# Gathers for three instead of four destination tiles in the second attention layer, with a ring of eight row sets

## The chip, the cores and the metric

The kernel runs on one core of a Trainium2 chip. The metric is the device time of one execution in microseconds (us); of several executions the median is given. The profile is one further execution, recorded by the hardware profiler. Its engines are PE (matrix products, with PEld for the loading of weights), DVE (vector), ACT (scalar), POOL (GpSimd) and SP, which only issues transfers.

## What is computed

A graph of 3125 nodes with 256 features and 103125 edges, sorted by destination, goes through four blocks in float32: three attention layers over the graph, a layer of 16 experts, a sum over neighbours, and a layer of 8 experts. The change touches the second of the three attention layers. One such layer is

```python
h = x @ W
el = h @ al
er = h @ ar
e = leaky_relu(el[src] + er[dst], 0.2)
m = segment_max(e, dst)
ex = exp(e - m[dst])
alpha = ex / segment_sum(ex, dst)[dst]
out = segment_sum(alpha[:, None] * h[src], dst) + b      # relu after layers 1 and 2
```

so every destination node takes a weighted mean of the rows of `h` of its source nodes.

## The kernel before

The nodes are cut into 25 tiles of 128 (the last has 53). The kernel has two ways to make the weighted sums of a layer.

The dense way serves all destinations of layers 1 and 3, and most of layer 2. The number of edges between each source and each destination lies in a table `counts`. Destinations are taken in parts of 256 (`PARTS_OF`; the last part has 53), and for each part the loop over `s` goes through the 25 source tiles. In step `s` DVE makes `pm` (L1575), the 128 x 256 weights of this source tile for these destinations, and PE multiplies each half of it with the 257 columns of `h` (features and the sum of weights) into `acc` (L1578), one matmul for each destination tile. The `pm` tiles come from a pool of six buffers. The part of 53 destinations has its own form (L1566, L1570). When a part is done, `divide` (L1610) makes the mean of it, and `onward_steps` (L1468) turns the result (L1474, L1476), multiplies it with the next layer's weights (L1345) and keeps it (L1352): a part's closing work is done by events placed in the steps of the next part.

The other way is `Apart` (L2050), used in layer 2 for the first destinations, here four tiles (0 to 3, 512 nodes). During layer 1 each row of `h` is also saved to a table in DRAM (L2063). For every destination the list of its sources lies in order in the edge list, so POOL fetches with one indirect transfer the j-th source row of 128 destinations at once: one row set of 128 x 258 values. A destination has 38 such slots (`OWN`), and up to 128 destinations with more edges get 20 extra ones (`HEAVY`), which are done first. DVE adds a row set times a coefficient into `apart_acc` (L2200); the coefficients of a batch of four slots come from one small instruction (L2191), which reads the four row sets. At the end of a tile the sums of the extra slots are handed out by a matmul (`expand`, L2205) and added (`gather`, L2209), and the tile goes onward as the others do.

Layer 2 is written out by hand in order (`manual_schedule`, L1527), so what stands before what on an engine is what the loops say. PE, DVE, ACT and POOL each run their own instructions in order. The parts of the layer are `NEXT_PARTS` (L1267): ten parts of 256 and the one of 53, and each engine's share of the gathers is laid into their steps by a plan: `events` (L2174) makes a list of pairs, a step number and what to do there. `at(q)` (L2179) turns the time of slot `q`, which is `LANDED + EVERY * q` (19.0 and 1.31 us), into a step, counting 0.976 us for a full step and 0.25 for one of the small part. The main loop runs the events that are due at the end of each step (L1593).

The row sets live in a ring of five buffers of four (`RING`). Five batches are fetched in one go at step 11 (L1588). After that a batch is fetched by four gathers, once the last slot of a batch has been added and has freed its buffer (L2218).

Around the change, SP carries in layer 2 only the saving of rows and weights for later, and POOL the gathers and a few small copies before and after them. Layer 3 begins with source tile 4 (L1573), so the rows of tiles 0 to 3 are wanted last.

Of the kernel before, what the change touches and what calls it, by code (L numbers as in the profile page):

```python
# [22 lines left out]
P = 128  # L23
# [1240 lines left out]
SOME = 6  # L1264
ROW = D + 2
APART = 2
NEXT_PARTS = PARTS_OF[APART:11] + PARTS_OF[12:] + PARTS_OF[11:12]  # L1267
FEW = 2 * APART
OWN = 38
HEAVY = 20  # L1270
SLOTS_OF = [(FEW, HEAVY)] + [(t, OWN) for t in range(FEW)]
BATCH_OF = 4
BATCHES_OF = [(t, k, min(BATCH_OF, n - k)) for t, n in SLOTS_OF for k in range(0, n, BATCH_OF)]
RING = 5
LANDED = 19.0
FETCH = 11
BEGIN = 0
RANK = [(5, 0), (5, 4), (5, 6), (5, 9), (5, 14), (5, 17), (6, 8)]
EVERY = 1.31
STEP, LAST_STEP = 0.976, 0.25  # L1280
HELD = 64.0


# [75 lines left out]
def dense_attention(tc, dram, counts, x_in, big, ident, eps, layers, src, dst, rows, high, make_router, over, count,  # L1359
# [11 lines left out]
    with tc.tile_pool(name="dw", bufs=1) as cp, tc.tile_pool(name="dwl", bufs=2) as wl, \  # L1371
# [3 lines left out]
        with tc.tile_pool(name="dp", bufs=6) as pmp, tc.tile_pool(name="ds", bufs=2) as sp, \  # L1375
# [120 lines left out]
            for i in range(3):  # L1496
# [14 lines left out]
                if apart_now:  # L1511
                    hold = ExitStack()
                    hp = hold.enter_context(tc.tile_pool(name="hp", bufs=1))
                    raws[0] = hp
                    hq = hold.enter_context(tc.tile_pool(name="hq", bufs=1, space=PSUM))
                    def finished(t, acc, b=bt_i, nxt=nxt, w=we_n):
                        col = hp.tile([P, 1], F32, name="apart_col", bufs=2)
                        nc.vector.tensor_scalar(col, acc[:, D:], 1e-30, None, op0=OP.max)
                        nc.vector.reciprocal(col, col)
                        nc.vector.scalar_tensor_tensor(acc[:, :D], acc[:, :D], col, b, op0=OP.mult, op1=OP.add)  # L1520

                        soon.extend(onward_steps(now_step[0] + 1, lambda: acc, t, P, "yT1", nxt, w, None))

                    now_apart += apart.events(finished)
                order = ExitStack()
                if apart_now:
                    order.enter_context(tc.manual_schedule())  # L1527
# [1 line left out]
                for here, (a, c, n) in enumerate(parts):  # L1529
                    tiles = [(q, (c + q) // P, min(P, n - q)) for q in range(0, n, P)]  # L1530
                    following = parts[here + 1:here + 2]
                    short = bool(following) and following[0][2] <= P // 2

                    edges = counts_of(counts, a)
                    if c > GROUPS[a][0]:
# [12 lines left out]
                    for s in range(NT):  # L1548
                        now_step[0] = here * NT + s
                        if s == (EARLIER if apart_now else TERMS):  # L1550
                            if following:
                                tau_next = terms(now, following[0])
                            else:
                                tau_next = None if last else terms(nxt, PARTS_OF[0 if apart_now else APART])
                        if i == 0 and (a, s) in FINISH:
                            locator.finish(FINISH.index((a, s)) + 1, pp)
                        if i == 0 and (a, s) in FIND:
                            locator.find(FIND.index((a, s)) + 1, kp, tau[:, 0:1])
                        later.sort(key=lambda e: e[0])
                        while later and later[0][0] <= s:  # L1560
                            later.pop(0)[1]()
                        if n <= P // 2:
                            if s % SOME == 0:
                                m = min(SOME, NT - s)
                                few = sp.tile([P, SOME, n], F32, name="few")
                                nc.vector.tensor_tensor(few[:, :m], tau[:, None, :n].to_broadcast([P, m, n]),  # L1566
                                                        now.rho[:, s:s + m, None].to_broadcast([P, m, n]), op=OP.max)
                                nc.vector.tensor_tensor(few[:, :m], few[:, :m], edges[:, s:s + m, :n], op=OP.mult)
                            at = s % 2 * (P // 2)
                            nc.tensor.matmul(acc[at:at + n, 0, :D + 1], few[:, s % SOME], now.h[:, s, :D + 1], start=(s < 2),  # L1570
                                             stop=(s >= NT - 2))
                        else:
                            of = (s + FEW) % NT if last and a == 0 else s  # L1573
                            pm = pmp.tile([P, PAIR], F32, name="pm")
                            nc.vector.scalar_tensor_tensor(pm[:, :n], tau[:, :n], now.rho[:, of:of + 1],  # L1575
                                                           edges[:, of, :n], op0=OP.max, op1=OP.mult)
                            for j, (q, t, r) in enumerate(tiles):
                                nc.tensor.matmul(acc[:r, j, :D + 1], pm[:, q:q + r], now.h[:, of, :D + 1], start=(s == 0),  # L1578
                                                 stop=(s == NT - 1))
                        if last and (a, s) == (2, 0):  # L1580
                            during(expert.a[:, 0, 0:1])
                        while ready and ready[0][0] <= s:
                            counter.add(kp, ready.pop(0)[1])
                        if i == 0 and (a, s) in prepare:
                            prepare[a, s]()
                        if apart_now and (a, s) == (APART, BEGIN):
                            apart.begin(hp, hq, pp, now.lr)
                        if apart_now and (a, s) == (APART, FETCH):  # L1588
                            for b in range(RING):
                                apart.fetch(b)  # L1590
                        while soon and soon[0][0] <= now_step[0]:
                            soon.pop(0)[1]()
                        while now_apart and now_apart[0][0] <= now_step[0]:  # L1593
                            now_apart.pop(0)[1]()
                        if s == 2 and fills:

                            for e in empties:
                                nc.gpsimd.tensor_scalar(e, tau[:, 0:1], 0.0, None, op0=OP.mult)
                        if s % 8 == 2 and fills:
                            fills.pop(0)()  # L1600
                        if ahead and s % 3 == 0:
                            counter.make(ahead[0], ACT_OH, tau[:, 0:1] if a == 0 and s < 6 else None)
                            ready.append((s + 2, ahead.pop(0)))
# [446 lines left out]
class Apart:  # L2050
# [86 lines left out]
    def begin(self, hp, hq, pp, lr):  # L2137
# [2 lines left out]
        numbers = hp.tile([P, P], F32, name="numbers")  # L2140
        nc.gpsimd.iota(numbers, pattern=[[1, P]], base=0, channel_multiplier=0, allow_small_or_imprecise_dtypes=True)
        self.numbers = numbers
        hot = hp.tile([P, BATCH_OF, ROW], F32, name="apart_row", bufs=RING)
        hot = hot.rearrange("p j f -> p (j f)")[:, :FEW * P].rearrange("p (t j) -> p t j", j=P)
        self.hots(hot)
        self.back = hp.tile([P, FEW, P], F32, name="hotT")
        ps = pp.tile([P, FEW, P], F32, name="ps_m")
# [11 lines left out]
        for t, n in SLOTS_OF:  # L2159
            nc.vector.tensor_scalar(self.real[:, c:c + n], numbers[:, :n], self.ends[:, t, 1:2], None, op0=OP.is_lt)  # L2160
            c += n
        self.ring = {}

    def fetch(self, b):
        nc = self.nc
        row = self.hp.tile([P, BATCH_OF, ROW], F32, name="apart_row", bufs=RING)
        q = sum(m for _, _, m in BATCHES_OF[:b])
        for j in range(BATCHES_OF[b][2]):
            nc.gpsimd.indirect_dma_start(  # L2169
                out=row[:, j], out_offset=None, in_=self.table[:, :],  # L2170
                in_offset=bass.IndirectOffsetOnAxis(ap=self.who[:, q + j:q + j + 1], axis=0))
        self.ring[b] = row

    def events(self, finished):  # L2174

        nc, made = self.nc, []
        state = {}

        def at(q):  # L2179
            time, steps = LANDED + EVERY * q, 0  # L2180
            for _, _, n in NEXT_PARTS:
                step = STEP if n > P // 2 else LAST_STEP
                if time < NT * step:
                    break
                time, steps = time - NT * step, steps + NT
            return steps + math.ceil(time / step)

        def batch(b, t, q, m):
            row = state["row"] = self.ring.pop(b)
            co = state["co"] = self.hp.tile([P, BATCH_OF], F32, name="apart_co", bufs=2)  # L2190
            nc.vector.scalar_tensor_tensor(co[:, :m], row[:, :m, D + 1], self.tau[:, t:t + 1], self.real[:, q:q + m],  # L2191
                                           op0=OP.max, op1=OP.mult)
# [14 lines left out]
        def gather(t):  # L2207
            acc = state["acc"]
            nc.vector.tensor_tensor(acc, acc, state["ps"], op=OP.add)  # L2209
            finished(t, acc)  # L2210

        q = 0
        for b, (t, k, m) in enumerate(BATCHES_OF):
            made.append((at(q + m), lambda b=b, t=t, q=q, m=m: batch(b, t, q, m)))
            for j in range(m):
                made.append((at(q + m + j), lambda j=j, first=(k + j == 0): slot(j, first)))
            if b + RING < len(BATCHES_OF):
                made.append((at(q + m + m - 1), lambda b=b: self.fetch(b + RING)))  # L2218
            if t < FEW and k == 20:
                made.append((at(q + m + m - 1), lambda t=t: expand(t)))  # L2220
            q += m
            if k + m == dict(SLOTS_OF)[t]:
                if t == FEW:
                    made.append((at(q + m - 1), lambda: state.update(heavy=state["acc"])))
                else:
                    made.append((at(q + m - 1), lambda t=t: gather(t)))
        return made


def spare_rows(tc, cp, rows0, rows1):  # L2230
# [148 lines left out]
```

## Time and profile before

| | |
|---|---|
| median of 3 runs | 1810.56 us (1809.9 to 1813.63) |
| the profiled execution, its own time | 1872.49 us |
| its span, first to last instruction | 1870.8 us |
| PE busy | 1768.7 us, 95% of the span |
| DVE busy | 1021.9 us, 55% |
| POOL busy | 488.6 us, 26% |
| mean granted clock of PE | 0.979 |
| gathers of layer 2 (L2169) | 172, 176.1 us busy on POOL |
| additions of row sets (L2198, L2200) | 172, of which 167 of 482 ns in the median |

The page of a profile gives for each engine how long it was busy, and the span in slices. Groups of instructions have a line of the kernel, an engine, an operation, what it writes and reads, a count, the busy time, the mean duration, and what ended the idle time before them. The view of waits says who waited for whom and for how long; the timeline lists instructions in order. A matmul of float32 leaves two records. The granted clock is the share of full speed that PE was allowed.

### The profile page before, as it was taken

What the parts mean: (1) busy time and instruction counts of PE and PEld (TensorE: products, weight loads), DVE (VectorE), ACT (ScalarE), POOL (GpSimd) and SP (SyncE); (2) the same over time, 40 slices, a digit from 0 to 9 for tenths busy, and PEclk for the clock granted to TensorE, in tenths of its full rate; (3) what the DMA queues carried; (4) which work ended last, traced back from release to release, by engine and by line L of the source; (5) the groups of instructions that cost most, each with busy time, mean ns of one, the idle gap of its engine ahead of it and who ended that gap; (6) DMA issues with size and microseconds to landing.
All of it is one profiled execution on the core that took longest, in us unless ns stands there. A gap on an engine that the chain in (4) does not pass through costs nothing. (4 is left out here: it accounts for less than half of the span.)

```text
span 1870.8 us, 27224 instructions
## 1 busy us (share of the span) xinstructions
PE 1768.7 (95%) x9196; PEld 1380.7 (74%) x9196; DVE 1021.9 (55%) x2933; ACT 727.8 (39%) x2079; POOL 488.6 (26%) x634
## 2 busy tenths in 40 slices
PE   6999999999698978999999999999989999999997
PEld 4788888887586866788887866666668887455786
DVE  6888888875476756777777842222244222333221
ACT  3766667671011111122222322121127999455221
POOL 4210110000566656123333333333310000122121
PEclk9999999999799989999999999999989999999999
DMA  4111123757323322211111177876430000723884
GB/s 116 33 38 56 61 68 136 311 225 300 81 77 82 84 74 79 91 38 46 46 46 41 46 223 195 234 195 194 111 88 1 1 1 1 236 116 154 265 293 124
DMA packets 123716, 215.45 MB, mean 115 GB/s; under 512 B 14811, under 2 KB 86657, under 8 KB 123528
## 3 DMA queue, kind: packets, MB, share of 16 engines
q1 hardware_dynamic: 85860, 137.38, 21.7%
q0 software_dynamic: 24704, 56.84, 11.5%
q10 hardware_dynamic: 12994, 19.29, 3.1%
q8 instruction: 79, 1.29, 0.3%
q14 instruction: 79, 0.65, 0.1%
HBM read 122.54 MB, written 92.61 MB: 115 GB/s over the span
## 5 line engine op out<-in xcount | busy, mean ns | idle before, releaser
L1578 PE MATMUL acc<-big,pm 128*128 128x257 f32 x3400 | 800.1, 386 | 18.9 <-issue 9.1
L1578 PEld LDWEIGHTS acc<-big,pm 128*128 128x128 f32 x3400 | 634.0, 192 | 113.3 <-DVE pm L1575 14.1
L1575 DVE SCALAR_TENSOR_TENSOR pm<-tau,big,counts 128x256 f32<-128x256 f32 (+1 forms) x875 | 400.3, 476 | 144.4 <-PE acc L1578 113.4
L2169 POOL DMA_INDIRECT apart_row<-apart_rows,apart_who x172 | 176.1, 1024 | 115.3 <-DVE apart_acc L2200 53.6
L1778 PE MATMUL acc<-msg,cr 128*128 128x512 f32 (+1 forms) x625 | 157.9, 404 | 0.0
L891 PE MATMUL ps_h<-xsT,w 128*128 128x384 f32 x448 | 147.3, 487 | 0.0
L1778 PEld LDWEIGHTS acc<-msg,cr 128*128 128x128 f32 (+1 forms) x625 | 114.7, 185 | 29.2 <-ACT cr L1774 1.2
L1774 ACT ACTIVATE cr<-counts 128x256 fp32r<-128x256 uint8 (+1 forms) x325 | 130.6, 402 | 13.6 <-PE acc L1778 6.8
L2035 ACT CAST counts<-acc_c 128x500 uint8<-128x500 f32 (+1 forms) x155 | 95.9, 677 | 95.0 <-PE acc_c L2025 94.7
L891 PEld LDWEIGHTS ps_h<-xsT,w 128*128 128x128 f32 x448 | 84.7, 190 | 58.0 <-issue 1.9
L2010 DVE TENSOR_TENSOR ohk<-iota_k,key 128x2016 f16<-128x2016 f16 (+1 forms) x79 | 94.3, 1194 | 20.2 <-PE acc_c L2025 20.0
L1345 PE MATMUL ps_m<-we,yT 128*128 128x258 f32 (+1 forms) x248 | 72.9, 415 | 31.3 <-ACT yT L1476 23.8
L894 ACT ACTIVATE silu<-ps_h 128x384 f32<-128x384 f32 x60 | 29.4, 490 | 170.4 <-PE ps_h L891 168.3
L2004 ACT ACTIVATE ohs<-iota_s,low 128x128 f16<-128x128 f16 x286 | 94.1, 401 | 0.0
L1056 PE MATMUL ps_H<-big,t_w 128*128 128x512 f32 (+1 forms) x224 | 93.1, 552 | 0.8 <-ACT H L1058 0.5
L1476 ACT ACTIVATE yT<-ps_m 128x256 f32<-128x256 f32 (+1 forms) x24 | 9.0, 374 | 212.4 <-remote 99.8
L895 DVE TENSOR_TENSOR hid<-silu,ps_h 128x384 f32<-128x384 f32 x60 | 33.2, 553 | 104.7 <-PE ps_h L891 104.7
L911 POOL DMA_INDIRECT sums<-y,who x45 | 70.0, 1556 | 72.9 <-DVE y L909 64.0
L1184 PE MATMUL ps_y<-t_wd,hsT 128*128 x384 | 87.1, 379 | 0.4 <-ACT hsT L1232 0.4
L2025 PEld LDWEIGHTS <-ohs 128*128 128x128 f16 x1250 | 77.7, 98 | 10.9
L2025 PE MATMUL acc_c<-ohk,ohs 128*128 128x125 f16 x1250 | 84.5, 218 | 0.0
L1345 PEld LDWEIGHTS ps_m<-we,yT 128*128 128x128 f32 (+1 forms) x248 | 45.9, 199 | 49.4 <-ACT yT L1476 26.8
(424 smaller groups left out, 2245.7 us busy)
## 6 DMA issues: line engine op xcount, KB each, us to landing
rows<-empty SPq DMA_DIRECT2D x16, 2564.0 KB
big<-in_L_ffn_w_dram SPq DMA_DIRECT2D x36, 512.0 KB
w<-in_L_ffn_w_dram ACTq DMA_DIRECT2D x36, 512.0 KB
hs<-rows SPq DMA_DIRECT2D x23, 641.0 KB
rows<-empty SPq DMA_DIRECT2D x16, 516.0 KB
t_wd<-in_L_ffn_Wd_dram SPq DMA_DIRECT2D x8, 1024.0 KB
big<-in_L_ffn_Wd_dram SPq DMA_DIRECT2D x6, 1024.0 KB
xs<-rows SPq DMA_DIRECT2D x14, 387.0 KB
```

The source lines that it names most:

```text
L891: nc.tensor.matmul(ps, w[:, k, j * P:(j + 1) * P], xsT[:, k], start=(k == 0), stop=(k == KD - 1))
L1056: nc.tensor.matmul(ps[:, :n], a[:, k, j * P:(j + 1) * P], xnT[:, k, c:c + n], start=(k == 0), stop=(k == KD - 1))
L1345: nc.tensor.matmul(ps[:r], xT[:, k], w[:, k], start=(k == 0), stop=(k == KD - 1))
L1575: nc.vector.scalar_tensor_tensor(pm[:, :n], tau[:, :n], now.rho[:, of:of + 1], edges[:, of, :n], op0=OP.max, op1=OP.mult)
L1578: nc.tensor.matmul(acc[:r, j, :D + 1], pm[:, q:q + r], now.h[:, of, :D + 1], start=(s == 0), stop=(s == NT - 1))
L1774: nc.scalar.activation(cr[:, :n], edges[:, s, :n], AF.Copy, accum_out=seen[:, a * NT + s:a * NT + s + 1])
L1778: nc.tensor.matmul(acc[:r, j].rearrange("p h d -> p (h d)"), cr[:, q:q + r], msg[:, s].rearrange("p h d -> p (h d)"), start=(s == 0), stop ...
L2004: nc.scalar.activation(far[:, i], self.iota_s, AF.Abs, scale=-1.0, bias=self.low32[:, batch, i:i + 1])
L2010: nc.vector.tensor_tensor(to[:, i:tiles].rearrange("p t (x u) -> p t x u", u=2), iota.rearrange("p (x u) -> p x u", u=2)[:, None].to_broad ...
L2025: nc.tensor.matmul(acc[:, u], ohs[:, i], ohk[:, i, :KEYS], start=(t == 0), stop=(t == TW - 1))
L2035: nc.scalar.copy(to[:, :, d0 % PAIR:d0 % PAIR + whole * WIN].rearrange("p s (u d) -> p u s d", u=whole), acc[:, :whole])
L2169: nc.gpsimd.indirect_dma_start(out=row[:, j], out_offset=None, in_=self.table[:, :], in_offset=bass.IndirectOffsetOnAxis(ap=self.who[:, q ...
```

## The change

Three tiles are fetched for (0 to 2, 384 nodes) in place of four. Tile 3 becomes a part of its own of 128 destinations, which layer 2 takes on the dense way as its second part: 25 steps with a half-wide `pm` and one matmul each. `FOLLOWED` names the extra slots and the first three tiles, so there are 134 gathers and additions, not 172, in 35 batches, not 45. The lists of sources and what is prepared from them still cover four tiles.

The ring becomes one tile with places for two batches (eight row sets, before twenty). The first eight row sets are no longer fetched in one go: each has an event of its own from step 11 on, `EVERY` apart, and behind a POOL copy of one column of the latest `pm` into `pace`, which holds it until that product has been made. Every later row set is fetched by an event right after the addition that frees its place, for the batch after the next; the last addition of a batch fetches what is left. The plan changes with it: `LANDED` 16.5, `EVERY` 1.74, and 0.3 us for a step of the 128-wide part. `made` is kept from running out of order, and the first fetches are sorted into it. The closing work of a part that the 128-wide part follows is placed as it is before the part of 53 (`short`).

```diff
-NEXT_PARTS = PARTS_OF[APART:11] + PARTS_OF[12:] + PARTS_OF[11:12]
+NEXT_PARTS = PARTS_OF[APART:APART + 1] + [(1, 3 * P, P)] + PARTS_OF[APART + 1:11] + PARTS_OF[12:] + PARTS_OF[11:12]
...
-BATCHES_OF = [(t, k, min(BATCH_OF, n - k)) for t, n in SLOTS_OF for k in range(0, n, BATCH_OF)]
-RING = 5
-LANDED = 19.0
+FOLLOWED = SLOTS_OF[:4]
+BATCHES_OF = [(t, k, min(BATCH_OF, n - k)) for t, n in FOLLOWED for k in range(0, n, BATCH_OF)]
+RING = 2
+LANDED = 16.5
...
-EVERY = 1.31
-STEP, LAST_STEP = 0.976, 0.25
+EVERY = 1.74
+STEP, HALF_STEP, LAST_STEP = 0.976, 0.3, 0.25
...
-                    now_apart += apart.events(finished)
+                    now_apart += apart.events(finished, lambda: pm[:, 0:1])
...
-                    short = bool(following) and following[0][2] <= P // 2
+                    short = bool(following) and following[0][2] <= (P if apart_now else P // 2)
...
-                        if apart_now and (a, s) == (APART, BEGIN):
+                        if apart_now and (here, s) == (0, BEGIN):
                             apart.begin(hp, hq, pp, now.lr)
-                        if apart_now and (a, s) == (APART, FETCH):
-                            for b in range(RING):
-                                apart.fetch(b)
...
-        hot = hp.tile([P, BATCH_OF, ROW], F32, name="apart_row", bufs=RING)
-        hot = hot.rearrange("p j f -> p (j f)")[:, :FEW * P].rearrange("p (t j) -> p t j", j=P)
+        self.rows = hp.tile([P, RING * BATCH_OF, ROW], F32, name="apart_row")
+        hot = self.rows.rearrange("p j f -> p (j f)")[:, :FEW * P].rearrange("p (t j) -> p t j", j=P)
...
-    def fetch(self, b):
+        self.pace = hp.tile([P, 1], F32, name="pace")
+
+    def of(self, b):
+        at = b % RING * BATCH_OF
+        return self.rows[:, at:at + BATCHES_OF[b][2]]
+
+    def fetch(self, b, j, behind=None):
         nc = self.nc
-        row = self.hp.tile([P, BATCH_OF, ROW], F32, name="apart_row", bufs=RING)
-        q = sum(m for _, _, m in BATCHES_OF[:b])
-        for j in range(BATCHES_OF[b][2]):
-            nc.gpsimd.indirect_dma_start(
-                out=row[:, j], out_offset=None, in_=self.table[:, :],
-                in_offset=bass.IndirectOffsetOnAxis(ap=self.who[:, q + j:q + j + 1], axis=0))
-        self.ring[b] = row
+        if behind is not None:
+            nc.gpsimd.tensor_copy(self.pace, behind)
+        q = sum(m for _, _, m in BATCHES_OF[:b]) + j
+        nc.gpsimd.indirect_dma_start(
+            out=self.of(b)[:, j], out_offset=None, in_=self.table[:, :],
+            in_offset=bass.IndirectOffsetOnAxis(ap=self.who[:, q:q + 1], axis=0))
+
+    def first(self, b, j, recent):
+        self.fetch(b, j, recent())
...
+        first = [(when(FETCH * STEP + g * EVERY),
+                  lambda b=g // BATCH_OF, j=g % BATCH_OF: self.first(b, j, recent)) for g in range(RING * BATCH_OF)]
         q = 0
         for b, (t, k, m) in enumerate(BATCHES_OF):
             made.append((at(q + m), lambda b=b, t=t, q=q, m=m: batch(b, t, q, m)))
+            ahead = range(BATCHES_OF[b + RING][2] if b + RING < len(BATCHES_OF) else 0)
             for j in range(m):
                 made.append((at(q + m + j), lambda j=j, first=(k + j == 0): slot(j, first)))
-            if b + RING < len(BATCHES_OF):
-                made.append((at(q + m + m - 1), lambda b=b: self.fetch(b + RING)))
+                for h in (ahead[j:j + 1] if j < m - 1 else ahead[j:]):
+                    made.append((at(q + m + j), lambda b=b, h=h: self.fetch(b + RING, h)))
...
-        return made
+        for k in range(1, len(made)):
+            made[k] = max(made[k][0], made[k - 1][0]), made[k][1]
+        return sorted(first + made, key=lambda e: e[0])
```

More of the change, by code (lines that the diff above doesn't have):

```diff
@@ L2161, in begin, with events @@
             c += n
-        self.ring = {}
-    def fetch(self, b):
-        nc = self.nc
-        row = self.hp.tile([P, BATCH_OF, ROW], F32, name="apart_row", bufs=RING)
-        q = sum(m for _, _, m in BATCHES_OF[:b])
-        for j in range(BATCHES_OF[b][2]):
-            nc.gpsimd.indirect_dma_start(
-                out=row[:, j], out_offset=None, in_=self.table[:, :],
-                in_offset=bass.IndirectOffsetOnAxis(ap=self.who[:, q + j:q + j + 1], axis=0))
-        self.ring[b] = row
-    def events(self, finished):
+        self.pace = hp.tile([P, 1], F32, name="pace")
[3 more added lines that the diff above has]
+    def fetch(self, b, j, behind=None):
+        nc = self.nc
+        if behind is not None:
[6 more added lines that the diff above has]
+        self.fetch(b, j, recent())
+    def events(self, finished, recent):
         nc, made = self.nc, []
@@ L2179, in at, with when @@
         def at(q):
-            time, steps = LANDED + EVERY * q, 0
+            return when(LANDED + EVERY * q)
+        def when(time):
+            steps = 0
             for _, _, n in NEXT_PARTS:
-                step = STEP if n > P // 2 else LAST_STEP
+                step = STEP if n > P else HALF_STEP if n > P // 2 else LAST_STEP
                 if time < NT * step:
@@ L2188, in batch @@
         def batch(b, t, q, m):
-            row = state["row"] = self.ring.pop(b)
+            row = state["row"] = self.of(b)
             co = state["co"] = self.hp.tile([P, BATCH_OF], F32, name="apart_co", bufs=2)
```

## The prediction

> **What bounds the kernel now.** I read first the busy time of the engines stage by stage: the three attention layers are 72 to 448, 456 to 786 and 786 to 1078 us of the span. Columns: length, then busy us (instructions) of PE, PE weight loads, DVE, ACT and POOL, granted clock, DMA share, GB/s.
>
> ```profile
> 72.00:448.00 376.00, 373.16 (x2651) 321.59 (x2649) 305.33 (x585) 246.76 (x643) 32.72 (x44) 1.00 0.37 139
> 456.00:786.00 330.00, 279.98 (x1264) 229.16 (x1263) 214.37 (x588) 40.39 (x140) 180.09 (x186) 0.93 0.28 77
> 786.00:1078.00 292.00, 289.34 (x1446) 246.64 (x1446) 220.85 (x814) 69.93 (x141) 87.31 (x171) 1.00 0.17 53
> ```
>
> Layers 1 and 3 are full on PE at full clock. Layer 2, the one that the change touches, leaves PE idle for 50 us and has a mean clock of 0.93. No other stage has a gap like it, so next comes the unit of PE work, from the chain that ended last (layer 3), and then the layer's gathers (count, then least, median and most ns, first and last start).
>
> ```profile
> 1063.44 5.65 PE acc L1578 x26
> ```
>
> ```profile
> L2169 POOL DMA_INDIRECT apart_row<-apart_rows,apart_who x172: 951/957/1287, 474.8 to 754.5; - x172
> L2200 DVE SCALAR_TENSOR_TENSOR apart_acc<-apart_row,apart_co,apart_acc x167: 469/482/533, 483.7 to 776.9; 128x257 f32<-128x257 f32 x167
> ```
>
> 26 records take 5.65 us, 0.217 each, and a matmul leaves two: 0.434 us for one destination tile and one source tile. At that price layer 2 is 250 full steps x 2 x 0.434 = 217, the 25 steps of the 53-wide part 10.9, onward work of 25 tiles (4 matmul records and 2 transposes of 0.109) 27, tau terms and the start 7: about 262 us of PE work in 330. The loss is 68.
>
> Where it sits is in the waits of this layer (us in total, times, longest) and the timeline of one stall.
>
> ```profile
> POOL apart_row L2169 <- DVE apart_acc L2200: 53.6, 16, 7.6
> ...
> PE ps_m L1345 <- ACT yT L1476: 23.8, 7, 7.3
> ...
> PE acc L1578 <- issue: 9.1, 4, 4.3
> ...
> PE acc L1578 <- DVE pm L1575: 7.0, 5, 3.6
> ```
>
> ```profile
> 721.00 0.38 PE L1474 MATMUL ps_m<-ident,y 128*128 128x128 f32 x2
> ...
> 721.22 1.03 PE L1578 MATMUL acc<-big,pm 128*128 128x257 f32 x4
> ...
> 726.06 0.95 POOL L2169 DMA_INDIRECT apart_row<-apart_rows,apart_who  x1 [0.30 <-issue]
> 729.10 0.38 ACT L1476 ACTIVATE yT<-ps_m 128x256 f32<-128x256 f32 x1 [11.57 <-remote]
> ...
> 729.53 2.09 PE L1345 MATMUL ps_m<-we,yT 128*128 128x258 f32 x4 [7.28 <-ACT yT L1476]
> ...
> 733.68 0.95 POOL L2169 DMA_INDIRECT apart_row<-apart_rows,apart_who  x1 [6.67 <-DVE apart_acc L2200]
> ```
>
> The ACT copy needs only the two transposes, over by 721.4, yet starts at 729.1, when the run of back-to-back gathers has been over for 2 us. PE stands behind it, and POOL then waits for the additions that DVE could not make. The signal from PE arrives late while POOL issues without a pause; neither a gather's data nor DVE's work is what is missing. The other large stalls (515, 664, 694) look the same.
>
> **What of this is in the median.** This matters more than the change itself. The profiled execution took 1872.49 us (span 1870.8), the median is 1810.56: 61.9 less. Stages that are full on PE at granted clock 1.00 cannot be that much shorter. PE's idle time outside layer 2 is 52 us (span less 1768.7 busy, less the 50), most of it at the start, at DMA waits between stages and at the end. The only place with 62 us to give is layer 2, whose loss is 68. So an execution that isn't profiled seems to have some 6 us of it left. The Trainium skill (Runtime: NRT & Kernel Launch, the preamble/postamble breakdown) says that a profile's total holds about 6.2 us that the reported time does not. Here the two differ already by 1.7 us between span and time. By the row layer 2 keeps 6 us of loss in the median, by the rule 12. I allow for 12, since the DMA waits elsewhere may shrink a little too. By the naive reading (68 us lost in the median as well) the change would be worth tens of us; that is a rival below.
>
> **The change, part by part.**
> Tile 3 goes back to PE: 25 steps of one matmul, 25 x 0.434 = +10.9 us, plus one tau transpose, 0.1. Its expansion matmul (0.43) goes; the onward work of the tile is the same by either way. PE: **+10.5 us**, in the engine that is full. No cover: a step of PE in a layer that is PE-bound is paid whole.
> DVE: 38 additions of 0.482 (-18.3), 10 coefficient instructions of 0.215 (-2.2), the combining ones of a tile (-1.2), against 25 half-width products of 0.316 (+7.9) and a division of 0.8: -13 of 214. DVE has 116 us idle in the layer, so this buys nothing by itself. In the half part a step costs 0.32 of DVE against 0.434 of PE, and an addition comes every six steps: PE stays ahead as the bound.
> POOL: 134 gathers for 172. One takes 0.957 + 0.30 = 1.26 us, so 217 us become 169; of a layer of about 270 us that is 80% before and 60% after. In the plan an addition comes every 1.74 us instead of 1.31, so POOL is busy 72% of the stretch in which it fetches, not 96%, and runs of gathers break up. This is what the relief comes from.
> Eight copies that pace the first gathers: no such row in the trace; the nearest is POOL's L1598 tensor_scalar, 0.43 to 0.45 us. 8 x 0.75 with the issue is 6 us of POOL, in 14 us of plan together with the 10 us of gathers. Behind them are queued only further gathers. A product buffer can't be rewritten before the copy has read it, but there are six buffers and a step is 0.87: 5.2 us of cover against some 2. The rule against it: SBUF — State Buffer (who interferes with whom) says that a DVE instruction with two SBUF inputs and a GpSimd instruction that reads SBUF exclude each other. By the rule up to 8 x 0.45 = 3.6 us of DVE; by the row DVE waits 0.38 us for PE in each of these steps, 9 us over 24 steps. So nothing either way, unless DVE were late there already: 0, bounds 0 and 3.6.
> The wait that is added: each refill stands in POOL's queue behind the addition that frees its place, with 8 places, not 20. Behind the refill are only refills. Who waits is the coefficient instruction of the batch after next, and with it all of DVE's products and PE. The price of a fetch: the fourth gather leaves POOL at 479.63 and the instruction that reads all four starts at 481.76, so 0.3 + 0.96 + 2.1 = 3.4 us. The lead: the last refill is issued five slots ahead, 5 x 1.74 = 8.7 us; where a batch of two lies between (twice), three slots, 5.2 us; behind a batch of two, three gathers at once need 5.9 of 12. All are covered, by 1.8 us at the worst place. Bounds: 0, and 2 us at each of the 35 batches if DVE runs late. I take 1. It can't gain.
> SP and ACT issue the same DMAs and none is moved past. The last addition falls on step 17 of the last part, before on step 19 or so: the start of layer 3 is not later.
> Relief: of the 6 to 12 us of loss in the median some must stay (layer 3, without gathers, has 3). Bounds 0 and 9; I take 6, by the POOL duty, which falls below three quarters. Sum: +10.5 + 1 - 6 = **+5.5 us**, 1816. For a profiled execution itself: PE work 272, and a loss that falls from 68 to perhaps 28, so 1872 + 10.5 - 40 = about 1843. The two sums differ in sign, and I hold to the one that fits the median.
>
> **The rivals.**
> As above, a PE-bound layer with more PE work, relief small: 1812 to 1822, likeliest 1816. Chance 0.47.
> The stalls are in the median too (other side): the late signals of PE during runs of gathers also hit executions that aren't profiled. For it: the granted clock of 0.93 is real, and the stalls repeat in each part. Against it: the 61.9 us have no other home. If 15 to 20 us of these come from DMA stretches elsewhere, the median keeps 20 to 30 us of loss in layer 2; thinner gathers give back 20, and +10.5 + 1 - 20 is -8.5: 1802; it decides as soon as the relief passes 11.5. Down to 1790. Chance 0.20.
> The ring of eight is too short: DVE works in bursts, so that additions come later than planned and the refill is late at most batches. From a lead under 3.4 us it costs; at 0.4 us for each of 35 batches, +14 and hardly any relief: 1826, up to 1840. Against it: 1.8 us to spare at the tightest place. Chance 0.15.
> The change doesn't do what it says: the half part hides in gaps that PE has anyway, and added and saved cancel: 1808 to 1813. Chance 0.18.
>
> **How the numbers follow.** A measurement of this kernel tells about 0.2% (3.6 us) from no change: under 1806.9 is faster, over 1814.2 slower. The first case falls over that line but for its lowest part, the third wholly: slower 0.60. The fourth and the low end of the first: same 0.20. The second: faster 0.20. The range leaves out half of the second case and the top of the third: 1800 to 1828; the likeliest case alone is 1812 to 1822.
>
> **What would show it.** In the profile after: layer 2's step still 0.87 us; 25 half steps at 0.434, some 11 us in all; POOL's waits for additions now at nearly every gather and harmless; waits of PE for the ACT copy well under 23.8 us; granted clock over 0.93 and the profiled execution nearer to the median, 1830 to 1855. Wrong would be: DVE's coefficient instruction waiting for a gather in most batches (the third case), or a median below 1807 (then the loss was in the runs).

## The result and the profile after

Over 11 runs each, the changed kernel takes 1816.54 us (1813.34 to 1822.85) and the kernel before 1806.75 us (1803.77 to 1813.63). The ratio is 1.0047, 95% interval 1.0034 to 1.006: about 8.5 us slower (0.0047 x 1806.75), 6.1 to 10.8; the two medians lie 9.8 us apart. In three of the four sets of runs that follow, on two chips, the kernel before is about as fast as here (1808 to 1811 us in the median). In the fourth, on a third chip, it takes 1864.64 us (35 runs, 1846.99 to 1873.79), and there the change is faster: ratio 0.9758, 0.9736 to 0.9781, told below.

The profiled execution of the changed kernel took 1813.34 us (span 1811.6). Its layers 1, 2 and 3 by stretches, columns as before:

```profile
66.80:451.30 384.50, 381.64 (x2711) 325.96 (x2713) 310.22 (x601) 249.41 (x655) 32.67 (x52) 1.00 0.39 146
451.30:720.00 268.70, 265.37 (x1277) 225.31 (x1274) 198.56 (x549) 38.68 (x136) 144.37 (x148) 1.00 0.27 75
720.00:1019.00 299.00, 296.91 (x1485) 254.87 (x1484) 226.50 (x835) 71.15 (x146) 87.48 (x174) 1.00 0.16 51
```

Layer 2 is now as full as the others: 3.3 us of PE idle time and a clock of 1.00, for 50 us and 0.93. The part of 128 destinations in the timeline of PE (the two transposes at 486.42 are for the part behind it), then the gathers and additions of the layer, and its waits:

```profile
479.47 7.11 PE L1579 MATMUL acc<-big,pm 128*128 128x257 f32 x32
486.42 0.38 PE L1463 MATMUL ps_m<-ident,lr 128*128 128x128 f32 x2
486.64 4.07 PE L1579 MATMUL acc<-big,pm 128*128 128x257 f32 x18
```

```profile
L2171 POOL DMA_INDIRECT apart_row<-apart_rows,apart_who x134: 940/947/2077, 469.5 to 707.0; - x134
L2207 DVE SCALAR_TENSOR_TENSOR apart_acc<-apart_row,apart_co,apart_acc x130: 470/482/951, 479.0 to 716.2; 128x257 f32<-128x257 f32 x130
...
DMA to landing us min/median/max: 2.7/2.8/4.1
```

```profile
POOL apart_row L2171 <- DVE apart_acc L2207: 62.1, 47, 4.2
...
PE acc L1579 <- DVE pm L1576: 1.7, 2, 1.1
DVE apart_co L2198 <- DMA apart_row<-apart_rows,apart_who: 1.7, 2, 1.5
```

The 50 records (32 and 18) are the 25 half steps. The first 16 of them fill the 6.95 us from 479.47 to 486.42, so a half step takes the 0.434 us of the prediction, and 25 take 10.85. POOL waits for an addition at 47 of its gathers, and this costs next to nothing: the rows are late for DVE twice, by 1.7 us together (`DVE apart_co L2198 <- DMA apart_row`: 1.7, 2, 1.5).

Put beside the profile that the prediction was made from, this reads as 59 us gained. It isn't so in the medians. Which profile of the kernel before was the odd one had to be found out first.

### The profile page after: what moved, and what is told of

It reads as the page before. It is cut to its first block, busy times and chain, and to the rows that moved or that the text cites. A ratio compares the mean times of both kernels' runs of the same rounds, so it can differ in the third digit from the quotient of the medians.

```text
span 1811.6 us, 27336 instructions
## 1 busy us (share of the span) xinstructions
PE 1755.9 (97%) x9245; PEld 1381.9 (76%) x9245; DVE 1010.7 (56%) x2909; ACT 727.3 (40%) x2080; POOL 453.1 (25%) x604
## 3 DMA queue, kind: packets, MB, share of 16 engines
q0 software_dynamic: 22880, 51.82, 10.8%
## 5 line engine op out<-in xcount | busy, mean ns | idle before, releaser
L1576 DVE SCALAR_TENSOR_TENSOR pm<-tau,big,counts 128x256 f32<-128x256 f32 (+1 forms) x900 | 408.3, 475 | 99.3 <-PE acc L1579 91.6
L2171 POOL DMA_INDIRECT apart_row<-apart_rows,apart_who x134 | 139.3, 1039 | 100.9 <-DVE apart_acc L2207 62.1
L2023 PEld LDWEIGHTS <-ohs 128*128 128x128 f16 x1250 | 77.7, 98 | 10.8
L1184 PEld LDWEIGHTS ps_y<-t_wd,hsT 128*128 128x128 f32 x384 | 71.2, 191 | 8.9 <-ACT hsT L1232 0.4
L1785 DVE TENSOR_TENSOR y<-acc,y 128x256 f32<-128x256 f32 (+1 forms) x25 | 10.6, 424 | 119.5 <-ACT y L1784 119.5
L906 PE MATMUL ps_o<-w,hid 128*128 128x256 f32 x336 | 76.5, 380 | 0.0
```

Of the source, the lines that this page charges most:

```text
L1184: nc.tensor.matmul(ps[part], hsT[:, j, part], of(j), start=(j == 0), stop=(j == nh - 1))
L2023: nc.tensor.matmul(acc[:, u], ohs[:, i], ohk[:, i, :KEYS], start=(t == 0), stop=(t == TW - 1))
L2171: nc.gpsimd.indirect_dma_start(out=self.of(b)[:, j], out_offset=None, in_=self.table[:, :], in_offset=bass.IndirectOffsetOnAxis(ap=self.wh ...
```

## The experiments

The theory to be tested: layer 2 is full on PE in the timed runs, so the matmuls of tile 3 are what the change costs, less a small relief from fewer gathers. The rivals: the new way of fetching costs time; or layer 2 loses much in the timed runs too. All were timed against the kernel before on their own chip.

**The kernel before again** (no edit).

> The kernel before, unchanged. It asks whether the 50 us of PE idle time in its profiled layer 2 belong to the kernel or to that one execution. If the loss comes with being profiled while POOL issues gathers without a pause, this profile shows it again: layer 2 over 300 us and some 1870 in all, with a median at 1806. If that execution was an odd one, the profile now shows a layer 2 of 258 to 265 us, PE idle for less than 6 us in it, and about 1806 in all. Ratio to before 0.998 to 1.002 by either.

Ratio 1.0003 (0.9991 to 1.0016), and its profile is another one: layer 2 takes 263.0 us, 456.3 to 719.3.

```profile
456.30:719.30 263.00, 256.95 (x1232) 215.82 (x1229) 208.32 (x573) 38.51 (x134) 184.98 (x178) 1.00 0.35 94
```

```profile
DVE apart_co L2191 <- DMA apart_row<-apart_rows,apart_who: 21.2, 24, 1.8
...
POOL apart_row L2169 <- DVE apart_acc L2200: 5.2, 17, 0.3
...
PE acc L1578 <- DVE pm L1575: 3.9, 7, 0.8
```

PE is idle for 6.1 us (263.0 less 256.95). The rows come late in 24 batches, 21.2 us of waiting on DVE; of this no more than 3.9 us reaches PE as waiting for a `pm`, past the six buffers. Between the same two points layer 2 took 323.3 us in the prediction's profile (456.6 to 779.9). So 268.7 after stands against 263.0, not 323, and the change costs 5.7 us of layer 2 in two single profiles, 8.5 in the medians. This run showed that the 50 us need not come with being profiled, but not yet what they do come with.

**Before with only its first 20 gathers.**

```diff
-            row = state["row"] = self.ring.pop(b)
+            row = state["row"] = self.ring[b % RING]
...
-            if b + RING < len(BATCHES_OF):
-                made.append((at(q + m + m - 1), lambda b=b: self.fetch(b + RING)))
```

> The kernel before with only its first 20 gathers: the other 152 are left out and DVE adds the same 20 row sets again, so part of the computation is left out. It measures what the gathers cost in layer 2 in the timed runs. If layer 2 before is full on PE and the gathers are hidden (added PE work explains the change), the gain is 0 to 4 us, ratio 0.998 to 1.0. If gathers still cost it the 6 to 12 us that the prediction allowed for, 0.993 to 0.997.

In whole it is not to be read: its layer 2 has other results, the stages after layer 3, which work on them, took 1019 us in place of 793, and the ratio is 1.1221. Its layer 2 can be read: 257.8 us with 2.9 us of PE idle time.

```profile
455.80:713.60 257.80, 254.90 (x1231) 216.23 (x1228) 205.41 (x573) 38.54 (x134) 23.58 (x26) 1.00 0.07 18
```

All gathers but 20 gone, the layer is 5.2 us shorter (263.0 less 257.8), and idle time is 3.2 of it. That is the most that fewer gathers could give back on this chip; it lies between the two expectations.

**One half of the change: three tiles, fetched as before.** The edit is the change's part list, `FOLLOWED`, `short` and plan in the kernel before; `RING = 5` and `fetch` stay.

> Only one half of the change: three tiles by gathers, tile 3 on PE with the plan of the change (16.5 and 1.74 us), but rows fetched as before, four at a time into five buffers, the first twenty in one go. If the added PE work is the cause, it is as slow as the change: +8 to +11 us, 1.0045 to 1.006. If the way of fetching is the cause, it is near before: within 3 us, 0.998 to 1.002.

Ratio 1.0051 (1.0032 to 1.0071); layer 2 takes 268.6 us with 3.3 us idle. It is as slow as the whole change.

**The other half: four tiles, fetched as in the change.** The edit is the change with the part list, plan (19.0, 1.31) and four tiles of before.

> The other half: four tiles by gathers and no part of 128 on PE, as before (plan 19.0 and 1.31 us), but with the change's way of fetching: eight places, one row set behind each addition, the first eight paced. If the added PE work is the cause, it is within 3 us of before: 0.998 to 1.002. If the short ring makes the additions wait, it is slower by 5 us or more, and more than in the change, since the lead of three slots is 3.9 us here where 3.4 are needed: 1.004 to 1.015, with DVE's coefficient instruction waiting for gathers.

Ratio 0.9998 (0.9987 to 1.0009); layer 2 takes 262.1 us with 5.6 idle. The short ring and the refills one by one cost nothing that can be seen (by the interval 2.4 us less to 1.6 us more), even at 1.31 us a slot. With the run before it this settles it between the halves: the tile on PE, with its plan, is the cost, the way of fetching isn't.

**The change without 23 of the 25 steps of its new part.**

```diff
+                            if not (apart_now and n == P and 0 < s < NT - 1):
                                 of = ...; pm = ...; the product; the matmuls
```

> The changed kernel, with 23 of the 25 steps of the part of 128 left out, their products on DVE and their matmuls on PE; so tile 3 gets the sum over two source tiles only. It prices the added PE work in the whole time. If that work is the cause, the time falls by 23 x 0.434 = 10 us, to 1.0 us above before or to 3 us below it: ratio 0.998 to 1.001. If something else in the change costs the 8 us (the plan, the handover between parts), the time falls by less than 5 us: over 1.002.

Ratio 1.0037 (1.0024 to 1.0049), so the whole time fell by some 2 us only. By the words of the expectation that speaks against PE's work as the cause. The profile shows where the rest went. Layer 2 fell by 4.4 us (268.7 to 264.3), and in it one new gap of PE stands, where the additions and the division of the part before had lain beside the half steps:

```profile
485.74 2.51 PE L1580 MATMUL acc<-big,pm 128*128 128x257 f32 x5 [3.92 <-DVE pm L1577]
```

4.4 and this gap of 3.9 are 8.3 of the 10 us. The rest is the clock: from 485.4 on it was granted at 0.50 for 3.4 us, so that the first matmuls behind the gap take about 0.43 us a record for 0.217, which is some 1.7 us (an estimate, half of 3.4). So the sum closes at 10.0. The stages after layer 3 took 796.5 us for 793.0, with tile 3's other features; why was not looked into. The edit took away the cover of DVE's work too, and its time as a whole is a poor price of PE's work. The next is the better one.

**Before with the added matmuls alone**, run on two chips.

```diff
+                            if apart_now and here == 1:
+                                if s == 0:
+                                    spare = hq.tile([P, D + 1], F32, name="spare_ps")
+                                nc.tensor.matmul(spare, pm[:, :P], now.h[:, of, :D + 1], start=(s == 0), stop=(s == NT - 1))
```

> The kernel before, computing all it did, with one further matmul in each of the 25 steps of its second part, of the same shape and from the same operands, into a spare bank that nobody reads. That is the change's added PE work with nothing else of the change. If this work is paid whole, layer 2 is 9 to 11 us longer and the ratio to before 1.005 to 1.006, at or a little over the change's 1.0047. If PE's idle time in layer 2 (6.1 us) takes it in, 3 to 6 us and 1.0015 to 1.0035, and most of the change's loss lies elsewhere.

> The kernel before with 25 added matmuls once more. On the chip of the last runs, where before takes 1865 us and loses some 50 us of PE time in layer 2, the added work vanished (0.9992): there it fits into what PE loses. The question of the price is still open for a chip on which before takes about 1808. There: 1.004 to 1.006 and a layer 2 of 271 to 274 us if the work is paid whole; 1.0015 to 1.0035 if the 6 us of idle time take it in. Should before take 1865 here too, 0.997 to 1.0015 again.

Where before takes 1807.92 us: ratio 1.0036 (1.0025 to 1.0046), 6.5 us. Layer 2 is 271.9 us, 8.9 longer, and PE's idle time in it 4.6.

```profile
455.10:727.00 271.90, 267.29 (x1281) 226.68 (x1278) 208.98 (x572) 38.52 (x134) 184.13 (x178) 0.99 0.34 91
```

Busy time rose by 10.3 us (267.29 less 256.95); by the profile 1.5 of these fell into idle time, by the medians 4. Some 1.7 of the 8.9 are not work: behind a gap of 2.35 us the clock was granted at 0.50 for 3.4 us from 712.0 on, which `b_again` does not have in this layer. The ratio lies between the two bands that were expected, just above the lower one (1.0015 to 1.0035); the 271.9 us lie inside the 271 to 274 of the whole price, but not without these 1.7. So the matmuls are most of what the change costs, and their price is some 6.5 to 7.2 us (8.9 less 1.7), not 10.5.

On the other chip the same 25 matmuls cost nothing that can be seen: 0.9992 (0.9969 to 1.0015), in a layer 2 of 327.5 us.

**The change again, on that other chip.**

> The changed kernel once more, beside the others on one chip: layer 2 at 268 to 270 us with 3 to 4 us of PE idle, ratio 1.004 to 1.006 by each theory. Against the kernel with the added matmuls alone it gives the relief: if that is the 2.8 us by which PE's idle time differs between the profiles, the change is 2 to 4 us faster than before with the added matmuls; if the relief is the 6 us of the prediction, 5 to 7 us.

1818.74 us against 1864.64: ratio 0.9758 (0.9736 to 0.9781), against every expectation. First before with the added matmuls, then the change, layer 2 of each on that chip:

```profile
456.40:783.90 327.50, 284.79 (x1281) 232.73 (x1278) 208.27 (x573) 38.49 (x134) 178.82 (x178) 0.93 0.28 75
```

```profile
456.70:728.80 272.10, 266.06 (x1277) 224.59 (x1274) 198.79 (x548) 38.67 (x135) 143.04 (x148) 1.00 0.27 74
```

The first is the picture of the profile of before that the prediction used: some 43 us of PE idle, clock 0.93. It appears in every timed run of before there too (its 35 runs have granted clocks of 0.979 to 0.987, against 0.989 to 0.996 where it takes 1808 to 1811). So it belongs to the chip that a run falls on, or to its state in that one set of runs, and not to the profiling. Which chip the first profile came from is not on record. With the change the stall is gone, 6.0 us idle.

**Four tiles, twenty places, one by one.** Two plans: in the first all twenty first row sets are paced by a copy and the slots lie from 16.5 on, 1.345 apart; in the second they go in one go at step 11, without copies, and slots lie from 19.0, 1.33 apart.

```diff
-RING = 2
+RING = 5
```

> Four tiles by gathers as before, row sets fetched one by one behind the additions as in the change, with twenty places, and the additions laid evenly over the whole layer (16.5 and 1.345 us). The version that could beat both: no added PE work, and POOL fed earlier than a batch at a time. If refills that wait for a whole batch are what is left of the loss, it gains 1 to 3 us: 0.998 to 0.9995, PE idle under 5 us. If POOL's own 1.26 us for each of 172 gathers is, it equals before: 0.9995 to 1.001.

> Four tiles by gathers with twenty places; the first twenty in one go without the pacing copies, every later row set behind its own addition, and a slot every 1.33 us from 19.0. It takes from the slow version with twenty places the two things in which it differed from the others, the paced start and the early plan. If these made the additions wait there (PE idle of 16.9 us, all in its first 65 us), layer 2 is back at 260 to 263 with 4 to 6 us idle, ratio 0.998 to 1.001. If refills one by one are slower with twenty places for another reason, it stays over 1.004.

The first: 1.0071 (1.0054 to 1.0087), layer 2 275.4 us with 16.9 us of PE idle, the most of all profiles without the stall. Its waits:

```profile
PEld acc L1579 <- DVE pm L1576: 19.8, 13, 2.5
...
DVE pm L1576 <- POOL pace L2169: 15.4, 12, 1.9
PE acc L1579 <- DVE pm L1576: 14.9, 12, 2.1
```

Products wait for the pacing copies to let go of their buffers. The plan wants a copy every 1.345 us; in the trace they come 1.3 to 1.6 us apart between 472 and 483 us, and 2.6 to 2.8 from 486 on, where refills stand between them in POOL's queue. In the change, eight copies make DVE wait for 2.0 us. The second plan fell on the chip where before takes 1865 and gave 1.0024 (1.0009 to 1.0039) with 49.9 us idle, so whether it repairs the first elsewhere stays open. It does show that refilling one by one, into twenty places, does not remove the stall of that chip with four tiles:

```profile
659.82 0.27 PE L1475 MATMUL ps_m<-ident,y 128*128 128x128 f32 x1
...
666.02 0.96 POOL L2171 DMA_INDIRECT apart_row<-apart_rows,apart_who  x1 [0.30 <-issue]
668.09 0.38 ACT L1477 ACTIVATE yT<-ps_m 128x256 f32<-128x256 f32 x1 [11.05 <-remote]
668.53 2.09 PE L1346 MATMUL ps_m<-we,yT 128*128 128x258 f32 x4 [7.57 <-issue]
```

It is the same picture: a transpose is over at 660.1, gathers leave POOL in an unbroken row until 667.0, and the copy that needs only the transposes starts a microsecond after that row ends.

**Three tiles at before's pace**, fetched as before, run twice.

```diff
-EVERY = 1.74
+EVERY = 1.31
```

> Three tiles by gathers and tile 3 on PE, fetched as before (four at a time, five buffers), but planned at before's pace of 1.31 us a slot, not 1.74. It asks where the relief of the sum comes from. If POOL's issuing without a pause is what costs PE its few us of idle time in layer 2 (6.1 in the second profile of before, 3.3 with three tiles at 1.74), they come back here: PE idle 4.5 to 6 us in layer 2, ratio 1.0055 to 1.0075. If it is only the number of gathers, idle stays near 3.3 and the ratio at 1.0045 to 1.0055.

> Three tiles by gathers at before's pace of 1.31 us a slot. It tells on a chip where before takes 1865 us whether the pace of the gathers or their number makes PE lose time. If the pace does (POOL busy without a pause), it loses as before does for 134/172 of the stretch: some 35 to 45 us more than the change, 1850 to 1865, ratio 0.992 to 1.0. If four tiles in all are needed for it, it is as fast as the change there, 1815 to 1825, 0.975 to 0.98. On a chip where before takes 1808, 1.0045 to 1.0065 as before, which tells nothing new.

1.0052 (1.0034 to 1.0069) with 5.7 us idle the first time, 1.0076 (1.0051 to 1.0101) with 3.8 the second, where before takes 1810.54 and 1807.92. Two profiles of one kernel differ by 1.9 us of idle time, as much as the effect that was looked for, so what relief comes from the slower pace was not resolved. Both runs fell on a chip without the stall. So it was not told apart whether the slower pace, the smaller number of gathers or the ring of eight with its paced start takes the stall away. The added work of PE alone does not: `b_plus_half` has it.

## Why the prediction was right, and where it was not

The direction holds, and the size within 3 us: +8.5 us for +5.5. That 1816 was forecast and 1816.54 measured is luck in part: the forecast was added to the 1810.56 of three runs, and over 11 runs before takes 1806.75. Point by point:

The loss left in the median. The prediction took 61.9 us off the profile's loss of 68 and concluded that some 6 us are left in the runs to come. The second profile has 6.1 us of idle time. The agreement is close, though two sizes in the loss of 68 were off: its stretch of 330 us runs 6 us into layer 3 (323.3 by the marks of `b_again`), and its 262 us of PE work are 257 in that profile, which nearly cancels. The subtraction came out right; its reading did not. Said was that an execution that isn't profiled is spared the loss. The runs showed in its place that one chip has the loss in all its runs of before and others in none. On that chip the second rival (the stalls are in the median too) is what happens, and far past its 8.5 us: 45.9 us faster (1864.64 less 1818.74). The prediction allowed for 12 us, not 6, by the 6.2 us that the Trainium skill (Runtime: NRT & Kernel Launch, the preamble/postamble breakdown) puts between a profile's total and the reported time. Nothing of that size shows here between a profiled execution and the others: in `b_again` the profiled one took 1811.45 us, all of them 1804.86 to 1814.22, and in each a time lies some 1.7 us over its span.

The added work of PE, +10.5: 25 steps in 10.85 us in the trace, but 6.5 in the medians (4.5 to 8.3) where nothing else was changed. That gaps of a layer with 6 us idle take the rest in is the likely reason; the profile shows it for 1.5 us only. "Paid whole" was too much by a few us.

The relief of 6, bounds 0 to 9: mis-sized. By idle time it is 2.8 (6.1 less 3.3), by the medians none that can be seen: the change's 1.0047 is not under the 1.0036 of the matmuls alone, which come from another set of runs, and their intervals overlap. The price was too high and the relief too high by about as much, and that the errors cancelled to within 3 us is luck. POOL's duty did fall, and late rows with it (DVE's waits 21.2 to 1.7 us); but these waits had been taken in by the `pm` buffers.

The copies at nothing and the ring of eight at 1: borne out by `t3_ring5`, as slow without them, and by `t4_one_by_one` at 0.9998 with the tightest lead. A row set lands 2.8 us after its issue in the median, under the 3.4 that the lead was held against. A copy takes 0.19 us, not 0.43. Three of the eight fall beside a product or an addition of DVE. Two of these take 0.31 and 0.38 us, and beside the third an addition takes 0.49 us for 0.36: what the two engines keep from each other is tenths of a microsecond here, not the 3.6 us that was its bound. With twenty copies they do cost, through the buffers that they hold, so the zero is for eight only.

The profile after, forecast at 1843 with a loss of 28: 1813 with 3.3 us idle, under the 1830 to 1855 given as a sign. That sum started from a profile of the disturbed kind and guessed how much of it would go; on the chip where this could be measured all but 6.0 us go. Of the other signs, PE's waits for the ACT copy are gone as said (23.8 us, now none), and POOL waits for additions at 47 of 134 gathers, not at nearly every one.

What stays open: what about that chip makes the signals late beside gathers, and how few gathers, or how slow a pace, it takes so that no stall comes of it. Four tiles in rings of twenty have the stall with either way of fetching; the change, with three tiles, eight places and 1.74 us, does not.

## What to carry to other kernels

When a profile and the timed runs differ by more than the ends of the span explain, list which stages could hold the difference, and take a second profile before a stall in it is treated as the kernel's. Work moved onto an engine that is full is paid for the most part (here some 6.5 to 7.2 of 10.85 us), while a wait taken from an engine behind a deep buffer buys little, so count the two in the same unit: idle time of the full engine. A change that costs half a per cent on one chip may save 2.4% on another, so a kernel is timed on more than one.

## What the runs showed of the hardware

The same program took 1808 to 1811 us on two chips and 1865 on a third. Its gathers were as long either way: in layer 2 of the disturbed profile a gather takes 957 ns on POOL in the median and a packet of its rows 168 ns, in the undisturbed one (`b_again`) 963 and 160. What differs is when PE's completion is seen by others: 7.7 us late in the stall of the prediction and 8.0 in that of `t4_ring5_go`, in bursts some 2 us after a row of gathers ends. The traces hold 2129 records of the updates of PE's main semaphore (the counter by which it tells the others what it has done) for 2194 instructions that make one, against 2196 for 2194. The granted clock fell to 0.5 for spells of 3.4 to 23.9 us, which adds to the loss; four of the five begin 3.6 to 4.8 us after PE fell idle.

The records of that semaphore say more. In the four profiles of the disturbed kind (`before`, `b_plus_half`, `t4_ring5_go` and also `a_again`, the change), 98 to 151 of some 2200 updates have no record within 0.15 us of their matmul's end. Each of these matmuls ended while POOL was issuing an indirect transfer or at most 1.4 us after it, where only about a quarter of them lie. In the ten other profiles, with the same kinds of gathers, not one is late. So on that chip late signals go with gathers, in whichever layer these stand; the change still has 98 of them, and they no longer add up to a stall. By what path a gather holds a signal up, and why on that chip alone, no run shows.
